# Tridiagonal form of a 256 x 256 matrix: turning A x instead of A u in the narrow half, and small steps moved from VectorE to GpSimd

## The chip, the cores and the metric

One core of a Trainium2 chip runs the whole kernel in one launch, all in float32. The metric is the device time of one execution in microseconds (us), as the median of several runs. Engines: TensorE (PE in the profile; its weight loads are PEld), VectorE (DVE), ScalarE (ACT), GpSimd (POOL), and SyncE (SP), which issues the DMAs.

## The reference, cut to what matters

Two graph layers are applied to 64 matrices x of 256 x 256, with one 256 x 256 adjacency matrix.

```python
def layer0(h, adj, S, W1, W2, W3):          # S = adj, so the weighting is adj * adj
    for each of the three weights: h = (adj * S) @ (h @ W), relu after the first two

def layer1(features, A, W1, b1, W2, b2):
    deg = sum(A, axis=0) + sum(A, axis=1) - diagonal(A)
    d_inv_sqrt = where(deg > 0, rsqrt(deg), 0)
    L_norm = d_inv_sqrt[:, None] * (diag(deg) - A) * d_inv_sqrt[None, :]
    _, U = eigh(L_norm)
    h = relu((U.T @ features) @ W1 + b1)
    return U @ (h @ W2 + b2)

x = x + layer0(relu(layernorm(x)), adj, adj, ...)
x = x + layer1(relu(layernorm(x)), adj, ...)
```

The expensive thing beside the matmuls is `eigh`: all eigenvectors of one symmetric 256 x 256 matrix. It depends on adj alone, not on x, so it can run beside layer 0.

## The kernel before, in words

**Two kinds of work run side by side.** The class `Eigen` computes the eigenvectors: the normed Laplacian (`laplacian`), its tridiagonal form by 254 Householder reflections (`tridiagonalize`, line 439), the reflections gathered into one matrix (`reflections`), the eigenvalues and eigenvectors of the tridiagonal matrix by divide and conquer from 16 small blocks up (`leaves`, then `level` for 32, 64, 128 and 256), and the products that give U and its transpose. This is one long chain of small dependent steps, most of them on VectorE. The class `Layers` works on the 64 matrices x in 32 pairs; its layer 0 (`products` and `rows`) is mostly matmuls on TensorE with copies on ScalarE, and needs nothing of the chain. Its layer 1 needs U, so it comes last.

**The class `Pace` (lines 161 to 259) mixes them by hand.** While the kernel is built, it keeps a clock of its own for each engine, with a cost for each operation (class `Op`). For every operation of the chain it works out when its inputs are ready, adds `LATER` (line 169: 0.4 us for TensorE, 0.1 for ScalarE), and lets waiting operations of layer 0 in ahead of it as long as they start before that (`chain`, `fits`, `run`). So the order of TensorE and ScalarE is fixed in the program. The order of VectorE, GpSimd and SyncE is set by the compiler's list scheduler, by its own times and in general by program order among what is ready. What is left of layer 0 when the chain ends is run at the start of layer 1 (`layer1`, `pace.finish`). The last pair's final steps are held back until then.

**One step of `tridiagonalize`** (k = 0 to 253, lo = k + 1) takes the current column x of A (below the diagonal) both as a row spread over all partitions, `xr`, and as a column, `xc` (two columns for the two halves of 128 rows). Rows are slices lo to 255, so they get shorter. Its parts:

- beta. `tail` is the sum of squares behind the first element (on ScalarE in the wide half, on VectorE in the narrow one), `nn` the squared length, `s0` its root on ScalarE. `q` is half the sign; `qn` = q nn; `qs` = q s0; `nb` = qn / s0 + qs, which is beta with its sign. In the trace `nb` is named m<-rs,qn,qs.
- A x as a column: `xa`, one row product with a sum for each half of 128 rows (r<-A,xr).
- u = x + beta e1: `u1` is its first element, written into `xr`; `uc` is the column. A u = A x + beta times the column of A at lo (`rc`): `ac`.
- The column `ac` is turned to a row on TensorE: a transpose of the column spread over 128 columns, into the PSUM tile psB (`pu`); the column `rc` is turned into psA (`pr`). One transpose each in the narrow half, two each in the wide one.
- `none` guards against a zero tail (two GpSimd operations), `den` = alpha beta + none, and `gam` = 1 / den. In the trace gam is a column of z.
- `gc` and `gr`: minus gam times A u as column and row. `uau` = u A u is a row product with a sum over pu and xr (r<-psB,xr). `c`, `f`: scalars out of it.
- The next column of A after the update, as a row (`both`, then `xn`) and as a column (`xcn`: two operations and a product with the 0/1 matrix `lower`), so that the next step's beta can be begun before A is updated.
- The update of A by two products of a row and a column for each half (A<-wr,q,A and A<-xr,wc,A).

For lo < 128 (127 steps) both halves of the rows are alive: this is the wide half. From lo = 128 on (127 steps) only the second half is alive: the narrow half. The helper `aside` puts q, qn, qs, gg = gam gam and gu = gg u1 on GpSimd in the wide half and on VectorE in the narrow one. The helpers `stt`, `ts`, `tt` and `recip` issue VectorE operations, so in the profile nearly all of them have line 209, where `Pace.issue` makes the call; steps are found by the names of tiles.

## Time and profile before

| what | value |
|---|---|
| median of 3 runs | 2453.63 us (2453.24 to 2455.24) |
| the profiled execution: its own time, its span | 2454.8 us, 2453.0 us |
| mean granted clock of TensorE | 0.99 |
| busy share of the span: PE, DVE, ACT, POOL | 98%, 88%, 41%, 19% |
| instructions of PE, DVE, ACT, POOL | 9240, 13352, 2827, 1625 |
| tridiagonal stage | from about 16 to 1348 us |
| last layer-0 matmul before layer 1; first DMA of layer 1 | 2242.52 us; 2272.59 us |

How to read it: the page gives the busy time of each engine, and the span in 40 slices with the busy share of each in tenths. PEclk is the clock that TensorE was granted, in tenths. A group of instructions is a line with the operation, its tiles (out<-in), its shape and count, then busy time in us and the mean of one in ns, then the idle time of the engine just before them and what ended it. A timeline line gives start and duration in us. A table of windows gives for each stretch the length and sum, then the busy time of PE, PEld, DVE, ACT and POOL with their instructions, the granted clock, the DMA share and GB/s. VectorE's instructions overlap: the next one may start while the last one writes, so a row of 0.30 us can be followed 0.21 us later by another one that doesn't need it. The spacing of starts is therefore what an operation costs its queue.

### The profile page before, as it was taken

The page shows a single profiled execution, that of the slowest core. Times are in us where ns is not written, and L with a number is a line of the kernel's source. Part 1 is how long each engine was busy: PE and PEld are TensorE (multiplying, and loading weights), DVE is VectorE, ACT ScalarE, POOL GpSimd, SP SyncE. Part 2 cuts the span into 40 slices and gives each one's busy share as a digit, 9 for nine tenths or more (in the row PEclk, how much of TensorE's full clock was granted, in tenths as well). Part 3 has the DMA queues.
Part 4 walks back from the last instruction along what each step waited for, and adds up shares of the span by engine and source line. Part 5 has one row for each costly group of instructions (what it writes and reads, how often), then busy time and mean ns, then how long its engine had stood idle before and what let it go on. Part 6 is the DMA issues. An engine that isn't in the chain of part 4 may idle for free. (4 is left out here: it accounts for less than half of the span.)

```text
span 2453.0 us, 38673 instructions
## 1 busy us (share of the span) xinstructions
PE 2393.1 (98%) x9240; PEld 1588.8 (65%) x9240; DVE 2151.1 (88%) x13352; ACT 1012.7 (41%) x2827; POOL 474.4 (19%) x1625
## 2 busy tenths in 40 slices
PE   7999999999999999999999999999999999997899
PEld 4666666666666656666666566666666666665788
DVE  7999999999999999999999999899987888786333
ACT  4344444544444444434444433334444444432222
POOL 2434333333333111111111000000000000000443
PEclk9999999999999999999999999999999999998899
DMA  3000000000000000000000000000000000000576
GB/s 112 18 13 15 22 23 18 22 22 23 6 22 23 23 18 23 22 22 6 23 23 23 30 22 23 9 18 23 22 22 27 18 22 22 22 5 1 202 257 202
DMA packets 59401, 90.05 MB, mean 37 GB/s; under 512 B 5792, under 2 KB 42784, under 8 KB 59168
## 3 DMA queue, kind: packets, MB, share of 16 engines
q1 hardware_dynamic: 59168, 87.52, 10.7%
q8 instruction: 75, 1.23, 0.2%
q14 instruction: 158, 1.29, 0.2%
HBM read 47.13 MB, written 40.37 MB: 36 GB/s over the span
## 5 line engine op out<-in xcount | busy, mean ns | idle before, releaser
L209 PE MATMUL bank<-y,L_gnn_W 128*128 128x512 f32 (+3 forms) x2184 | 905.5, 566 | 0.0
L209 PEld LDWEIGHTS bank<-y,L_gnn_W 128*128 128x128 f32 x2184 | 402.5, 190 | 436.1 <-issue 414.9
L209 PE MATMUL bank<-L_gnn_W,s 128*128 128x256 f32 (+1 forms) x2108 | 464.6, 374 | 6.0 <-ACT s L209 6.0
L209 PEld LDWEIGHTS bank<-L_gnn_W,s 128*128 128x128 f32 x2108 | 390.3, 191 | 56.1 <-ACT s L209 7.0
L209 ACT ACTIVATE s<-bank 128x512 f32<-128x512 f32 x384 | 224.7, 586 | 188.9 <-PE bank L209 187.7
L209 PE MATMUL bank<-gt,s 128*128 128x256 f32 (+1 forms) x1040 | 231.5, 376 | 0.0
L209 PE MATMUL bank<-L_gnn_W,y 128*128 128x512 f32 (+3 forms) x532 | 230.6, 578 | 0.0
L209 PEld LDWEIGHTS bank<-gt,s 128*128 128x128 f32 x1040 | 194.0, 190 | 35.9 <-issue 10.3
L209 ACT ACTIVATE s<-nn,guard 128x1 f32<-128x1 f32 x254 | 74.6, 294 | 238.3 <-DVE nn L209 214.6
L209 ACT COPY y<-bank 128x512 f32<-128x512 f32 x192 | 111.0, 581 | 132.4 <-PE bank L209 131.6
L209 POOL COPY m<-xr 128x1 f32<-128x1 f32 x254 | 55.2, 217 | 561.3 <-DVE xr L209 554.4
L209 PEld LDWEIGHTS bank<-L_gnn_W,y 128*128 128x128 f32 x532 | 98.7, 191 | 97.8 <-issue 95.0
L209 ACT ACTIVATE h<-x,shift,scale 128x256 f32<-128x256 f32 x256 | 137.5, 590 | 54.7 <-DVE shift L209 54.6
L209 ACT ACTIVATE junk<-x,nm 128x256 f32<-128x256 f32 x256 | 129.0, 504 | 31.3 <-DVE nm L209 27.3
L209 DVE SCALAR_TENSOR_TENSOR A<-xr,wc,A 128x255 f32<-128x255 f32 (+63 forms) x381 | 139.5, 367 | 0.0
L209 ACT ACTIVATE junk<-x 128x256 f32<-128x256 f32 x256 | 105.6, 412 | 80.9 <-DVE x L209 69.2
L209 ACT ACTIVATE junk<-xr 128x254 f32<-128x254 f32 (+63 forms) x127 | 46.0, 362 | 224.8 <-DVE xr L209 218.8
L209 DVE SCALAR_TENSOR_TENSOR A<-wr,q,A 128x255 f32<-128x255 f32 (+63 forms) x381 | 138.7, 365 | 0.0
L209 DVE SCALAR_TENSOR_TENSOR q<-q 128x1 f32<-128x1 f32 (+1 forms) x576 | 119.7, 208 | 15.0 <-ACT q L209 4.7
L209 PE MATMUL bank<-gt,h 128*128 128x256 f32 (+1 forms) x526 | 122.0, 381 | 2.3 <-ACT h L209 2.2
L209 PE MATMUL bank<-p,gt 128*128 128x512 f32 (+1 forms) x264 | 117.7, 580 | 0.0
L209 POOL TENSOR_TENSOR xb<-x,ub 128x512 f32<-128x512 f32 x16 | 19.9, 1267 | 500.8 <-DMA hw<-hw 489.7
(615 smaller groups left out, 4356.0 us busy)
## 6 DMA issues: line engine op xcount, KB each, us to landing
x<-x SPq DMA_DIRECT2D x60, 512.0 KB, 3.4
x<-in_x_dram SPq DMA_DIRECT2D x64, 256.0 KB, 3.6
out_dram<-out SPq DMA_DIRECT2D x64, 256.0 KB, 2.2
hw<-hw SPq DMA_DIRECT2D x60, 256.0 KB, 2.7
L_gnn_W<-in_L_gnn_W_dram SPq DMA_DIRECT2D x1, 2048.0 KB, 10.0
L_gnn_W<-in_L_gnn_W_dram SPq DMA_DIRECT2D x1, 1024.0 KB, 12.5
L_gnn_W<-in_L_gnn_W_dram SPq DMA_DIRECT2D x1, 512.0 KB, 5.2
mask<-in_c_blk_dram SPq DMA_DIRECT2D x2, 256.0 KB, 2.6
```

The costliest lines, as they stand in the source:

```text
L209: return op.call(*op.args, **op.kwargs)
```

## The change

In the narrow half (lo >= 128) the column A x (`xa`) is turned to a row (`px`) as soon as it is there, beside the way to beta; formerly A u (`ac`) was turned, which needs beta. gam A u is then put together both as a row and as a column from gam A x and gam beta times the column of A: `gnb` = gam nb; row `px1` = px gam, `gr` = pr gnb + px1; column `ac` = xa gam, `gc` = rc gnb + ac. `uau` is taken from `gr`, so it holds one gam more, and `gg` is gam itself there.

In the wide half the turned column is A u, as before.

In both halves q, qn, u1, gu and the product of `xcn` with `lower` are GpSimd operations now (q, qn and gu were so in the wide half already; qs stays on `aside`). In the wide half den becomes two GpSimd operations. gr and gc hold plus gam A u, so ngam goes and several sums become differences. uc is written in the living half alone, and the rest of `us` is set to zero once, ahead of the loop. The GpSimd memset of xcn's first column goes. LATER for TensorE is 0.5 instead of 0.4.

```diff
--- before.py
+++ after.py
@@ -166,7 +166,7 @@
 
     WINDOW = 1.0
     SLOWER, IN_BLOCKS = 1.06, 1.13
-    LATER = {"PE": 0.4, "ACT": 0.1}
+    LATER = {"PE": 0.5, "ACT": 0.1}
     HOP = 0.5
     LEAD = 1.5
 
@@ -449,6 +449,7 @@
         drow, erow = self.row("D"), self.row("E")
         nc.vector.memset(erow[:, N - 1 : N], 0.0)
         nc.vector.memset(us[:, :, N - 2 : N], 0.0)
+        nc.vector.memset(us[:, 0, P - 1 : N - 2], 0.0)
         nc.vector.memset(gams[:, N - 2 : N], 0.0)
 
         def as_row(tag, column, halves):
@@ -486,8 +487,8 @@
             x1 = xr[:, lo : lo + 1]
             self.stt(nn, x1, x1, tail, OP.mult, OP.add)
             nc.scalar.activation(s0, nn, AF.Sqrt, bias=guard)
-            aside(lo).tensor_scalar(q, x1, 0.0, 0.5, OP.is_ge, OP.subtract)
-            aside(lo).tensor_tensor(qn, q, nn, OP.mult)
+            nc.gpsimd.tensor_scalar(q, x1, 0.0, 0.5, OP.is_ge, OP.subtract)
+            nc.gpsimd.tensor_tensor(qn, q, nn, OP.mult)
             return nn, s0, q, qn
 
         xc = self.col("xc")
@@ -507,53 +508,69 @@
             self.recip(rs, s0)
             aside(lo).tensor_tensor(qs, q, s0, OP.mult)
             xa, junk = self.col("xa"), self.row("r0")
-            for h in halves:
-                self.stt(junk[:, r], a[:, h, r], 1.0, xr[:, r], OP.mult, OP.mult, accum=xa[:, h : h + 1])
-                if h == halves[0]:
-                    self.stt(nb, rs, qn, qs, OP.mult, OP.add)
+
 
             ac, uc = self.col("ac"), us[:, :, k]
-            self.stt(ac[:, hs], rc[:, hs], nb, xa[:, hs], OP.mult, OP.add)
-            pu, pr = as_row("psB", ac, halves), as_row("psA", rc, halves)
+            times_x = lambda h: self.stt(
+                junk[:, r], a[:, h, r], 1.0, xr[:, r], OP.mult, OP.mult, accum=xa[:, h : h + 1]
+            )
+            times_x(halves[0])
+            if lo >= P:
+                px, pr = as_row("psB", xa, halves), as_row("psA", rc, halves)
+            self.stt(nb, rs, qn, qs, OP.mult, OP.add)
+            if lo < P:
+                times_x(1)
+                self.stt(ac[:, hs], rc[:, hs], nb, xa[:, hs], OP.mult, OP.add)
+                pu, pr = as_row("psB", ac, halves), as_row("psA", rc, halves)
 
             none = self.col("none", 1)
             nc.gpsimd.tensor_scalar(none, tail, 1e-30, 1e30, OP.is_le, OP.mult)
             nc.gpsimd.tensor_tensor(none, none, nn, OP.add)
-            den, ngam, gg, gu = (self.col(c, 1) for c in ("den", "ngam", "gg", "gu"))
+            den, gg, gu = (self.col(c, 1) for c in ("den", "gg", "gu"))
             gam = gams[:, k : k + 1]
             u1 = xr[:, lo : lo + 1]
-            self.ts(u1, u1, nb, OP.add)
-            self.stt(den, alpha, nb, none, OP.mult, OP.add)
+            if lo < P:
+                nc.gpsimd.tensor_tensor(den, alpha, nb, OP.mult)
+                nc.gpsimd.tensor_tensor(den, den, none, OP.add)
+            else:
+                self.stt(den, alpha, nb, none, OP.mult, OP.add)
+            nc.gpsimd.tensor_tensor(u1, u1, nb, OP.add)
             self.recip(gam, den)
-            self.stt(uc, ident[:, :, lo], nb, xc, OP.mult, OP.add)
-            self.ts(ngam, gam, -1.0, OP.mult)
-            aside(lo).tensor_tensor(gg, gam, gam, OP.mult)
-            aside(lo).tensor_tensor(gu, gg, u1, OP.mult)
+            self.stt(uc[:, hs], ident[:, hs, lo], nb, xc[:, hs], OP.mult, OP.add)
             gc, gr = self.col("gc"), row("gr")
-            self.ts(gc[:, hs], ac[:, hs], ngam, OP.mult)
 
             uau, c = self.col("uau", 1), self.col("c", 1)
-            self.stt(junk[:, r], pu[:, r], 1.0, xr[:, r], OP.mult, OP.mult, accum=uau)
-            self.ts(gr[:, r], pu[:, r], ngam, OP.mult)
+            if lo < P:
+                nc.gpsimd.tensor_tensor(gg, gam, gam, OP.mult)
+                self.ts(gc[:, hs], ac[:, hs], gam, OP.mult)
+                self.stt(junk[:, r], pu[:, r], 1.0, xr[:, r], OP.mult, OP.mult, accum=uau)
+                self.ts(gr[:, r], pu[:, r], gam, OP.mult)
+            else:
+                gg, gnb, px1 = gam, self.col("gnb", 1), row("px")
+                self.tt(gnb, gam, nb, OP.mult)
+                self.ts(px1[:, r], px[:, r], gam, OP.mult)
+                self.stt(gr[:, r], pr[:, r], gnb, px1[:, r], OP.mult, OP.add)
+                self.stt(junk[:, r], gr[:, r], 1.0, xr[:, r], OP.mult, OP.mult, accum=uau)
+                self.ts(ac[:, hs], xa[:, hs], gam, OP.mult)
+                self.stt(gc[:, hs], rc[:, hs], gnb, ac[:, hs], OP.mult, OP.add)
+            nc.gpsimd.tensor_tensor(gu, gg, u1, OP.mult)
 
             xn, xcn, both, f = row("xr"), self.col("xc"), self.row("r1"), self.col("f", 1)
-            self.stt(both[:, rest], gr[:, rest], u1, pr[:, rest], OP.mult, OP.add)
-            self.stt(f, uau, gu, gr[:, lo : lo + 1], OP.mult, OP.add)
-            self.stt(xn[:, rest], xr[:, rest], f, both[:, rest], OP.mult, OP.add)
+            self.stt(both[:, rest], gr[:, rest], u1, pr[:, rest], OP.mult, OP.subtract)
+            self.stt(f, uau, gu, gr[:, lo : lo + 1], OP.mult, OP.subtract)
+            self.stt(xn[:, rest], xr[:, rest], f, both[:, rest], OP.mult, OP.subtract)
             more = lo + 1 < N - 1
             if more:
                 alpha1, tail1 = below(xn, lo + 1)
             self.stt(c, uau, 0.5, gg, OP.mult, OP.mult)
             wr, wc = row("wr"), self.col("wc")
-            self.stt(wr[:, r], xr[:, r], c, gr[:, r], OP.mult, OP.add)
-            self.stt(wc[:, hs], uc[:, hs], c, gc[:, hs], OP.mult, OP.add)
+            self.stt(wr[:, r], xr[:, r], c, gr[:, r], OP.mult, OP.subtract)
+            self.stt(wc[:, hs], uc[:, hs], c, gc[:, hs], OP.mult, OP.subtract)
             if more and halves[0]:
                 following = length(xn, lo + 1, tail1)
-            if halves[0]:
-                nc.gpsimd.memset(xcn[:, 0:1], 0.0)
-            self.stt(xcn[:, hs], gc[:, hs], u1, rc[:, hs], OP.mult, OP.add)
-            self.stt(xcn[:, hs], uc[:, hs], f, xcn[:, hs], OP.mult, OP.add)
-            self.tt(xcn[:, hs], xcn[:, hs], self.lower[:, hs, lo], OP.mult)
+            self.stt(xcn[:, hs], gc[:, hs], u1, rc[:, hs], OP.mult, OP.subtract)
+            self.stt(xcn[:, hs], uc[:, hs], f, xcn[:, hs], OP.mult, OP.subtract)
+            nc.gpsimd.tensor_tensor(xcn[:, hs], xcn[:, hs], self.lower[:, hs, lo], OP.mult)
             if more and not halves[0]:
                 following = length(xn, lo + 1, tail1)
 
```

## The prediction

> **What bounds the kernel now.** I read the page's slices first: who is busy, and where does that stop?
>
> ```profile
> span 2453.0 us, 38673 instructions
> ...
> PE   7999999999999999999999999999999999997899
> ...
> DVE  7999999999999999999999999899987888786333
> ...
> PEclk9999999999999999999999999999999999998899
> ```
>
> TensorE is busy nearly everywhere, because layer 0's matmuls are poured into the gaps of the eigenvector chain, and VectorE, which carries that chain, is busy for nine tenths of the time until slice 37. Both look like the bound. The table of windows (span; then PE, PEld, DVE, ACT, POOL busy; clock; DMA) tells them apart: tridiagonal form, wide half; narrow half; the place where the chain ends.
>
> ```profile
> 100.00:700.00 600.00, 599.09 (x2382) 390.77 (x2381) 578.30 (x3119) 288.17 (x872) 226.70 (x795) 1.00 0.06 20
> 800.00:1340.00 540.00, 536.16 (x2086) 345.17 (x2085) 522.84 (x4151) 233.92 (x637) 93.58 (x488) 1.00 0.06 20
> ...
> 2243.00:2278.00 35.00, 14.60 (x35) 10.36 (x35) 10.65 (x44) 9.60 (x30) 0.29 (x1) 0.57 0.10 35
> ```
>
> In the third row the poured-in work has run out (the last such matmul starts at 2242.52) while the chain has about 30 us to go: TensorE does 14.6 us of work in 35, at a clock of 0.57. So the chain sets the time today, but only just. If the chain gets shorter by X in the tridiagonal stage, the matmuls that no longer fit there move behind and fill this hole. Idle there: 35 - 14.6 = 20.4 us; and the work in it runs at about half clock: 14.6 x (1 - 0.57) = 6.3 us, if it stayed warm. So **a gain of the chain counts up to some 20 to 27 us; after that TensorE's own work is the bound** (in 2300 to 2450 it is busy for 148.38 of 150). A loss of the chain counts in full.
>
> Next the chain's step. The tridiagonal stage has 127 wide steps (lo < 128, from 20 to about 775 us) and 127 narrow ones (to 1348). In a narrow step around 1007 us the timeline (start, duration) shows
>
> ```profile
> 1007.40 0.22 DVE L209 SCALAR_TENSOR_TENSOR ac<-A,m,xa 128x1 f32<-128x1 f32 x1
> ...
> 1008.11 0.15 DVE L209 TENSOR_SCALAR ngam<-z 128x1 f32<-128x1 f32 x1
> 1008.18 0.15 DVE L209 TENSOR_TENSOR gg<-z 128x1 f32<-128x1 f32 x1
> ...
> 1008.36 0.27 PE L209 MATMUL psB<-ident,ac 128*128 128x128 f32 x1
> ...
> 1008.55 0.22 DVE L209 SCALAR_TENSOR_TENSOR xc<-gc,xr,A 128x1 f32<-128x1 f32 x1
> ...
> 1008.69 0.24 DVE L209 SCALAR_TENSOR_TENSOR r<-psB,xr 128x82 f32<-128x82 f32 x1
> ```
>
> The turned row is there at 1008.63, yet its reader (r<-psB) starts at 1008.69, when the last small operation ahead of it has gone. VectorE's own queue ends last. In the wide half it is another queue:
>
> ```profile
> 405.04 0.47 POOL L209 TENSOR_SCALAR q<-xr 128x1 f32<-128x1 f32 x1
> ...
> 405.59 0.46 POOL L209 TENSOR_SCALAR none<-m 128x1 f32<-128x1 f32 x1
> ...
> 406.13 0.21 POOL L209 TENSOR_TENSOR qn<-q,nn 128x1 f32<-128x1 f32 x1
> ...
> 406.63 0.39 POOL L209 TENSOR_TENSOR qs<-q,s 128x1 f32<-128x1 f32 x1
> ...
> 407.05 0.22 DVE L209 SCALAR_TENSOR_TENSOR m<-rs,qn,qs 128x1 f32<-128x1 f32 x1
> ```
>
> Beta (m<-rs,qn,qs) starts 0.03 us after GpSimd's qs, and GpSimd has had hardly a gap since 405.04. Stepping through all wide steps without layer-norm work, the median of that distance is 0.03 us. VectorE was idle for only 0.07 us per step there (6.9 us over 99), so the page does not name GpSimd; but it releases beta.
>
> **Narrow half, part by part** (by spacing of starts in the step from 1002.73 to 1007.15, 4.43 us long; it ends at beta). Leaves VectorE for GpSimd: q (0.07), qn (0.12), the product with lower (0.07), u1 (0.12), gu (0.12). Dropped: ngam (0.07), and gg (0.12), since gam takes its place: 0.69 us. Added on VectorE: gnb = gam beta (a single small operation like ngam, 0.07), and a row px1 = px gam (like gr<-psB, 0.21); gr becomes a two-operand row (0.22 for 0.21). That is -0.40 us. Against it, px1, gr and uau are now in series. A row that needs the one before it starts 0.34 us later (xr at 1005.41, tail at 1005.75) where the queue alone would take 0.21, so two gaps of 0.13; the small ac, gc, which depend only on gam and gnb, fit into them. Filled, the step wins 0.40; with both gaps open 0.14. The transposes now start from xa, beside beta, den, gam and gnb (0.25 + 0.26 + 0.26 + 0.19 = 0.96 us from beta's start). From ac's end to the row in PSUM it takes 1.01 us in the step above; from xa's end (1007.23), with LATER raised by 0.1, that is 1008.34, against 1008.11 for gam times beta: TensorE's row may end last, by some 0.2, which takes back part of the gain. On GpSimd the step has 8 operations instead of 4, at 0.21 to 0.25 each (its means in 800 to 1340), 1.8 us of 4.1: room, but qn and none are now queued behind each other ahead of beta and den; 0 to 0.15. I take **-0.25 us a step** (ends -0.40 and -0.10): 127 x 0.25 = 32 us less. Nothing on SP or the DMA queues is touched; GpSimd issues no DMA in this stage.
>
> **Wide half.** VectorE loses den (0.13), u1 (0.12), ngam (0.07) and the product with lower (0.07): 0.39 us. Two places must be kept apart.
> From beta to the row's reader: den becomes two GpSimd operations, each 0.19 like gg, and a hop of about 0.08: gam starts some 0.85 us after beta's start, 1.05 if u1 is queued between them, for 0.81 now (401.89 - 401.08). Behind gam wait gg, gc, gr. VectorE's queue there gets shorter by 0.32, but the turned row lands only 0.18 us before its reader starts (mean of the steps without layer norm), and LATER gives 0.1 of this away. So -0.18 to +0.20; I take -0.10, nearest to the queue's rows.
> From the new row x to the next beta: GpSimd ends last, and the product with lower joins this queue. In program order it stands ahead of q and qn and of the next step's none and qs, so I expect it before qs. What does it cost there? The groups by shape in 100 to 700 give both ends:
>
> ```profile
> L209 POOL TENSOR_SCALAR q<-xr 128x1 f32<-128x1 f32 x100 | 45.0, 450 | 0.0
> ...
> L209 POOL TENSOR_TENSOR gg<-z 128x1 f32<-128x1 f32 x99 | 19.1, 193 | 120.4 <-DVE z L209 120.4
> ```
>
> The same one-element work takes 450 ns while VectorE runs its long rows (q ends at 405.51, just after the update of A at 405.01 that lasts 0.42) and 193 ns beside VectorE's short ones. In between lie none (364), qs (374) and qn (222), the tensor operations of this very stretch; I take 0.30, less the 0.09 of idle that the queue has ahead of none (8.7 us over 100): +0.21. It is 0 if it lands behind qs, +0.45 if it waits out a row. Together **+0.11 us a step** (ends -0.18 and, both bad ends, +0.65): 127 x 0.11 = 14 us more.
>
> The Trainium skill, "SBUF — State Buffer", section "Who interferes with whom", says that a VectorE instruction with two SBUF inputs and a GpSimd instruction that reads SBUF exclude each other, and that the one issued first blocks the other. One direction is the 450 ns above. The other, VectorE waiting for GpSimd, the trace does not show: the row r<-A,xr at 406.29 starts inside qn's span (406.13 to 406.34) and takes 0.35, its usual 346 ns. By the rule the four operations newly on GpSimd (den twice, u1, the product with lower, 0.19 each) could each hold a row up, an estimated 0.76 us a wide step and 97 us in all; I go by the row.
>
> **Small things.** The memset of us (128 x 127) runs once, ahead of the loop: under 0.5 us, as the row copies there take 0.42. uc in the narrow half is one column instead of two: nothing, both take 0.2. Signs turned from add to subtract: nothing. The GpSimd memset of xc in the narrow half (98 ns) goes; it was idle time. LATER 0.4 to 0.5 lets layer-0 matmuls in for 0.1 us longer ahead of each step's first transpose: up to 254 x 0.1 = 25 us where TensorE's row ends last. Today it is covered by the 0.37 us (narrow) and 0.18 us (wide) that the row lies ready before it is read; in the changed narrow step that cover goes, and this is in the -0.10 end above.
>
> **Sum.** -32 + 14 = -18 us, under the 20 to 27 that the hole can give back, so all of it shows. The profiled execution took 2454.8 us (span 2453.0 and 1.8 around it), 1.2 more than the median of 2453.63. 2454.8 - 18 = 2436.8; as a median, 2436 us.
>
> **Rivals.**
> The hole closes. Narrow -0.40 and wide 0 would be X = 51 us, of which 20 to 27 show: 2427 to 2434, or, with TensorE waiting a little less for its transposes in 254 steps (0.05 each, 13 us), 2420 to 2429; I say 2427. For it: VectorE's 97% in the narrow half. Against it: GpSimd's queue in the wide half.
> GpSimd becomes the bound (the slower side). In the wide half beta waits for qs already; if the product with lower costs a full 0.45 in front of it, or den through two GpSimd operations and u1 comes late, so that the step gains 0.40, that is 127 x 0.40 = 51 us more, and 51 - 32 = 19 us slower: 2473. It decides from a loss of 0.25 us a wide step, which eats the 32 us of the narrow half. For it: 0.03 us between qs and beta. Against it: the front part's shorter queue.
> The change does not do what it says. TensorE's order is fixed when the kernel is built, with layer-0 work filled in by the kernel's own clock; if the transposes stand as far apart as before, VectorE only waits where it worked, and the step stays: 2449 to 2458, say 2452. For it: the transposes start more than 0.17 us after ac's end in 132 of 220 steps, so TensorE's order is near the edge too. Against it: that clock counts VectorE's operations, and they become fewer.
>
> **How the numbers follow.** Forecast (2429 to 2448): 0.40. Hole closed (2418 to 2429): 0.24. No change (2449 to 2458): 0.12. GpSimd the bound (2459 to 2485): 0.24. Faster by over 0.2% (below 2449; 0.2% is about what a measurement of this kernel can tell from no change): 0.64; within 0.2%: 0.12; slower: 0.24. The range 2420 to 2470 leaves out some 0.04 below and 0.13 above.
>
> **What would show it.** Narrow half: beta to beta at about 4.1 instead of 4.4 us, the row px1 starting about 0.9 us after beta, VectorE below 97% busy. Wide half: the product with lower on GpSimd ahead of qs, beta still 0.03 us behind qs, the new row x to the next beta longer by 0.2 (2.6 now); gam at 0.85 or more after beta. The stage ends at about 1330 instead of 1348, and the window in which TensorE idles at half clock shrinks from 35 us to 15 or less. The prediction is wrong if the wide step grows by 0.25 or more, if the narrow one does not shrink, or if the stage ends earlier and the end does not follow.

## The result

The changed kernel takes **2495.62 us** (median of four runs, 2492.24 to 2496.5) where the kernel before takes 2453.48 beside it (four runs, 2453.24 to 2455.24). The ratio is 1.0168, with an interval of 1.015 to 1.0185: slower by 1.7%, where 0.7% faster was forecast. The time lies above the range that ended at 2470.

The page of the changed kernel first; the lines answer to those of the kernel before.

```profile
span 2492.3 us, 39259 instructions
...
PE 2404.4 (96%) x9220; PEld 1576.2 (63%) x9220; DVE 2127.3 (85%) x12210; ACT 1012.6 (41%) x2827; POOL 655.6 (26%) x2641
...
PE   7999999999999999999999899999999999999899
...
DVE  7999999999999999989998999999898888786333
...
PEclk9999999999999999999999999999999999999999
```

VectorE did lose work (12210 instructions, formerly 13352) and GpSimd gained it (2641, formerly 1625), as the diff says. But VectorE's share fell from 88 to 85% while the span grew: it now waits. Where, the table of windows tells, with the same three stretches as in the prediction.

```profile
100.00:700.00 600.00, 593.85 (x2336) 382.12 (x2335) 556.46 (x2709) 282.84 (x858) 288.63 (x1187) 1.00 0.06 20
800.00:1340.00 540.00, 508.98 (x1950) 320.44 (x1949) 491.11 (x3287) 211.15 (x573) 176.85 (x904) 1.00 0.05 18
2243.00:2278.00 35.00, 35.00 (x92) 17.24 (x91) 29.80 (x151) 12.71 (x34) 0.00 (x0) 1.00 0.00 1
```

In the second row, the narrow half, VectorE idles for 540 - 491 = 49 us (17 before) and TensorE for 31 (4 before): each waits for the other, and neither is busy throughout. In the third row TensorE, which stood idle for 20 of 35 us there, works without a gap: the chain now ends later, and layer-0 work that found no place in the narrow half is done here.

Cutting the trace at the first beta, at beta of the first narrow step and at the last beta gives the two halves of the stage. The same cuts for all runs (stages and span in us from the profiled execution; median and ratio against the kernel before, run beside it):

| kernel | wide half | narrow half | last beta at | span | median | ratio (interval) |
|---|---|---|---|---|---|---|
| before | 766.1 | 559.8 | 1346.2 | 2453.0 | 2453.48 | |
| **after** | 767.2 | **595.2** | 1383.7 | 2492.3 | 2495.62 | 1.0168 (1.015 to 1.0185) |
| later_only | 769.6 | 562.5 | 1352.1 | 2461.5 | 2462.2 | 1.0035 (1.0021 to 1.0049) |
| moves_only | 768.0 | 534.5 | 1323.9 | 2441.5 | 2442.71 | 0.9955 (0.9938 to 0.9972) |
| turn_only | 760.5 | 608.8 | 1390.6 | 2499.2 | 2500.11 | 1.019 (1.0173 to 1.0207) |
| after_later04 | 767.5 | 585.5 | 1372.8 | 2491.1 | 2493.86 | 1.0168 (1.0151 to 1.0185) |
| rows_first | 767.6 | 548.7 | 1337.0 | 2443.2 | 2445.19 | 0.9969 (0.9957 to 0.9982) |
| rows_first_late | 766.8 | 606.7 | 1393.4 | 2496.5 | 2498.78 | 1.0193 (1.0176 to 1.021) |
| after_late | 767.3 | 614.2 | 1403.1 | 2502.9 | 2505.78 | 1.0221 (1.0204 to 1.0238) |
| moves_narrow | 761.1 | 535.5 | 1317.7 | 2424.9 | 2427.03 | 0.9899 (0.9882 to 0.9915) |
| rows_first_wr | 768.1 | 550.4 | 1341.0 | 2450.6 | 2448.88 | 0.9979 (0.9969 to 0.9988) |
| extra_row | 760.2 | 542.6 | 1322.9 | 2433.0 | 2433.94 | 0.9918 (0.9901 to 0.9935) |
| **lower_wide** | 752.6 | 534.2 | 1308.4 | 2423.7 | **2424.93** | 0.9881 (0.9864 to 0.9897) |
| qs_vector | 765.5 | 534.7 | 1320.3 | 2429.1 | 2431.66 | 0.9911 (0.9894 to 0.9928) |
| turned_repaired | 752.6 | 545.7 | 1318.4 | 2429.3 | 2431.69 | 0.9912 (0.9895 to 0.9928) |
| den_wide | 768.1 | 533.2 | 1321.1 | 2436.8 | 2440.38 | 0.9947 (0.993 to 0.9963) |

Of the 39.3 us that the span grew, 35.4 are the narrow half's (127 steps, 0.28 each), 1.1 the wide half's.

Two things are needed to read the stages. Each length is from one execution; versions whose code and LATER are the same in a half agree there within 2.3 us (narrow half of moves_only, moves_narrow, lower_wide, qs_vector and den_wide: 533.2 to 535.5) and 1.3 us (wide half of the changed kernel, after_late and the three rows_first versions: 766.8 to 768.1). And a version also differs in how much layer-0 work `Pace` lets into a stage. Counted from the traces in units of a 128x512 matmul (a 128x256 one is half a unit; the transposes to psA and psB are left out), it is

| kernel | wide half | narrow half |
|---|---|---|
| before | 1618 | 1211 |
| after, rows_first | 1600 | 1190 |
| after_later04 | 1582 | 1160 |
| moves_only | 1582 | 1161 |
| moves_narrow | 1614 | 1164 |
| lower_wide | 1592 | 1160 |
| turned_repaired | 1592 | 1166 |
| den_wide | 1595 | 1157 |
| qs_vector | 1622 | 1156 |
| extra_row | 1614 | 1174 |
| turn_only | 1614 | 1248 |

of 5184 units in the whole kernel, later layers included. Work that isn't done in the stage is done behind it, at an estimated 0.43 us a unit (925.5 units from 1800 to 2200 us in the kernel before, with TensorE busy for 399.82 of these 400). So a shorter stage is a gain of the kernel only where TensorE has idle time left behind it.

One narrow step of the changed kernel shows what happens. First TensorE, then VectorE (start, duration):

```profile
1004.16 0.29 PE L209 MATMUL psB<-ident,xa 128*128 128x128 f32 x1 [0.40 <-DVE m L209]
```

```profile
1003.93 0.21 DVE L209 SCALAR_TENSOR_TENSOR m<-rs,qn,qs 128x1 f32<-128x1 f32 x1
...
1004.51 0.16 DVE L209 RECIPROCAL z<-den 128x1 f32<-128x1 f32 x1
1004.71 0.16 DVE L209 TENSOR_TENSOR gnb<-z,m 128x1 f32<-128x1 f32 x1
1004.78 0.21 DVE L209 TENSOR_SCALAR ac<-xa,z 128x1 f32<-128x1 f32 x1
1005.02 0.22 DVE L209 SCALAR_TENSOR_TENSOR gc<-A,gnb,ac 128x1 f32<-128x1 f32 x1
1005.35 0.22 DVE L209 SCALAR_TENSOR_TENSOR xc<-gc,xr,A 128x1 f32<-128x1 f32 x1
1005.48 0.30 DVE L209 TENSOR_SCALAR px<-psB,z 128x86 f32<-128x86 f32 x1
1005.89 0.31 DVE L209 SCALAR_TENSOR_TENSOR gr<-psA,gnb,px 128x86 f32<-128x86 f32 x1
1006.23 0.25 DVE L209 SCALAR_TENSOR_TENSOR r<-gr,xr 128x86 f32<-128x86 f32 x1
```

The turned A x is in PSUM at 1004.45, half a microsecond after beta's start: turning it early works, and gam (z) is the last thing px needs. By 1004.71 VectorE has started gnb, which needs gam too, so px could run here. It starts at 1005.48. Ahead of it stand ac, gc and xc, and gc and xc each wait for the one before (0.24 and 0.33 between starts, where independent ones follow at 0.07 to 0.13). The row waits behind small operations that wait. Then px, gr and r<-gr,xr (which gives uau) wait for each other in turn, and nothing small is left to fill these gaps.

That is no single step. Over all 126 narrow steps from beta to beta, px starts ahead of gc in 9, and ahead of xc in 15. Over the steps without layer-norm work the median of the row's landing is 0.52 us after beta and that of px's start 1.56. And the groups in 800 to 1340 show VectorE's new idle time in front of just these lines (the last number is the idle time before them):

```profile
L209 DVE SCALAR_TENSOR_TENSOR gr<-psA,gnb,px 128x126 f32<-128x126 f32 (+56 forms) x114 | 33.0, 289 | 10.1
...
L209 DVE SCALAR_TENSOR_TENSOR xc<-gc,xr,A 128x1 f32<-128x1 f32 x114 | 25.0, 219 | 10.4 <-DVE gc L209 0.5
```

In the kernel before, xc<-gc had 0.0 there, and no row more than 5.5. One could instead look at TensorE's waits in the same stretch and blame the transposes:

```profile
PE psB L209 <- DVE r L209: 14.3, 32, 1.5
PE psB L209 <- DVE m L209: 13.5, 38, 0.7
```

TensorE waits 28 us for xa (r<-A,xr; m starts beside it), where the kernel before shows 2.8 us of waiting for psB's input in all. So there are two theories: **VectorE's order** (the row is read late), and **TensorE's lost time** (or LATER, which let the transposes come when they do). A third, from the prediction, is that the operations moved to **GpSimd** cost more than they save.

### The profile page after: what moved, and what is told of

Read it like the earlier page. It is cut to its first block, busy times and chain, and to the rows that moved or that the text cites. A ratio compares the mean times of both kernels' runs of the same rounds, so it can differ in the third digit from the quotient of the medians.

```text
span 2492.3 us, 39259 instructions
## 1 busy us (share of the span) xinstructions
PE 2404.4 (96%) x9220; PEld 1576.2 (63%) x9220; DVE 2127.3 (85%) x12210; ACT 1012.6 (41%) x2827; POOL 655.6 (26%) x2641
## 3 DMA queue, kind: packets, MB, share of 16 engines
q14 instruction: 164, 1.34, 0.2%
## 5 line engine op out<-in xcount | busy, mean ns | idle before, releaser
L209 POOL COPY zn<-q 128x32 f32<-128x32 f32 x32 | 7.0, 218 | 423.3 <-DVE q L209 370.6
## 6 DMA issues: line engine op xcount, KB each, us to landing
L_gnn_W<-in_L_gnn_W_dram SPq DMA_DIRECT2D x1, 1024.0 KB, 14.2
```

Source lines behind the costliest of these rows:

```text
L209: return op.call(*op.args, **op.kwargs)
```

## The experiments

### The parts apart

**later_only**: the kernel before, with only

```diff
-    LATER = {"PE": 0.4, "ACT": 0.1}
+    LATER = {"PE": 0.5, "ACT": 0.1}
```

> The kernel before with LATER 0.5 instead of 0.4 for TensorE, nothing else. The narrow step of before reads its turned row 0.44 us after it lands (median), so 0.1 us more should be hidden. Theory 'row order' (the changed narrow step is slower because VectorE's queue puts three small operations ahead of the row px, and px, gr, uau then follow one another): 2453 within 5 us. Rival 'LATER' (the later transposes cost the time): 2470 or more, with the narrow step 0.1 us longer.

Measured: 2462.2 us. LATER alone costs some 9 us, spread over the wide half (+3.5), the narrow one (+2.7) and what follows. That is more than the 5 I had allowed and far less than the rival needs.

**after_later04**: the changed kernel with this one line undone.

> The changed kernel with LATER 0.4. In the compiled queue of VectorE the row px stands ahead of the column xc in 41 of 122 narrow steps here, in 13 with 0.5. Theory 'row order': a little better than the changed kernel, 0.02 to 0.08 us a narrow step, 2485 to 2494. Rival 'LATER': back to 2453 within 5 us. Rival 'hops': 2495, no difference.

Measured: 2493.86 us. The narrow half gets 9.7 us shorter and the last beta comes 10.9 us earlier, but the span is only 1.2 us shorter: LATER is not the cause. Nothing arrives at the end because TensorE's own work is the bound there. The stage holds 48 units less layer-0 work, an estimated 21 us, and in 2200 to 2400 us TensorE is idle for 10.0 us in the changed kernel (first row) and for 1.4 here (second):

```profile
2200.00:2400.00 200.00, 189.98 (x779) 143.05 (x778) 109.48 (x384) 62.47 (x147) 42.34 (x34) 0.97 0.31 103
2200.00:2400.00 200.00, 198.56 (x804) 145.60 (x803) 104.00 (x370) 70.06 (x169) 42.48 (x35) 1.00 0.33 109
```

So the changed kernel stands near both bounds: the chain still ends last in it, but leaves TensorE idle for only 10 us there.

**moves_only**: the changed kernel, but A u is turned in the narrow half as before, and LATER is 0.4. Only the small operations are on GpSimd.

```diff
-            if lo >= P:
-                px, pr = as_row("psB", xa, halves), as_row("psA", rc, halves)
...
-            if lo < P:
+            if True:
                 nc.gpsimd.tensor_tensor(gg, gam, gam, OP.mult)
                 self.ts(gc[:, hs], ac[:, hs], gam, OP.mult)
```

> The changed kernel with A u turned in the narrow half as before and LATER 0.4: only the small operations are on GpSimd, in both halves. Theory 'row order': the narrow step gets shorter by some 0.2 us (VectorE's queue loses seven small operations), the wide one by nothing to -0.05: 2425 to 2445. Rival 'hops' (the small operations on GpSimd put their hops into the narrow step's path and leave VectorE without anything to fill its gaps): narrow step 0.15 us longer or more, 2470 to 2490.

Measured: 2442.71 us, the narrow half 534.5 (25.3 less than before, 0.20 a step). Moving small operations off VectorE is the good half of the change; GpSimd's queue is not the trouble in the narrow half. The span gains 11.5 us here, and 28.1 where den, u1 and the product with lower stay on VectorE in the wide half (moves_narrow, below).

**turn_only**: the changed kernel with the small operations back where they were, and LATER 0.4: A x is turned, nothing else.

```diff
-            nc.gpsimd.tensor_scalar(q, x1, 0.0, 0.5, OP.is_ge, OP.subtract)
+            aside(lo).tensor_scalar(q, x1, 0.0, 0.5, OP.is_ge, OP.subtract)
...
-            nc.gpsimd.tensor_tensor(u1, u1, nb, OP.add)
+            self.ts(u1, u1, nb, OP.add)
```

> The changed kernel with LATER 0.4 and the small operations where they were before (den, u1 and the product with lower on VectorE; q, qn, gu, qs on VectorE in the narrow half): only the turning of A x is left. Theory 'row order': the narrow step is as long as in the changed kernel or longer, 4.7 to 5.0 us against 4.44 before: 2485 to 2520. Rival 'hops': narrow step no longer than 4.45: 2455 or less.

Measured: 2500.11 us, the narrow half 608.8 (49 more than before). The turning costs what the change loses: +49.0 here, and +51.0 from moves_only to after_later04. In the narrow half the two parts of the change simply add.

### VectorE's order, or TensorE's lost time

**rows_first**: the changed kernel with three orders added to VectorE's queue, in the narrow half: ac behind px, gc behind gr, the first operation on xc behind uau. `behind(late, early)` fixes an order in the queue and nothing else: no engine waits for another by it. row1 is px1, row2 gr, row3 uau, first the operation xc<-gc,xr,A.

```diff
-                self.ts(ac[:, hs], xa[:, hs], gam, OP.mult)
-                self.stt(gc[:, hs], rc[:, hs], gnb, ac[:, hs], OP.mult, OP.add)
+                behind(self.ts(ac[:, hs], xa[:, hs], gam, OP.mult), row1)
+                behind(self.stt(gc[:, hs], rc[:, hs], gnb, ac[:, hs], OP.mult, OP.add), row2)
...
+            if lo >= P:
+                behind(first, row3)
```

> The changed kernel with three orders added to VectorE's queue in the narrow half, and no other edit: ac goes behind px, gc behind gr, the first column operation of xc behind uau. In the changed kernel px starts 1.56 us after beta (median) though its row has landed at 0.52 and gam is there at about 0.75. Theory 'row order': px starts at about 0.9, the narrow step falls from 4.74 to 4.1 to 4.3, and the time to 2430 to 2450. Rival 'rows in series' (px, gr and uau each wait for the one before, and what is taken out in front of them comes back as gaps between them and behind): narrow step 4.55 to 4.75, 2475 to 2496.

Measured: 2445.19 us, the narrow half 548.7. The order alone is worth 595.2 - 548.7 = **46.5 us**, with the same layer-0 work in the stage (1190 units). VectorE in one of its steps:

```profile
1017.13 0.21 DVE L209 SCALAR_TENSOR_TENSOR m<-rs,qn,qs 128x1 f32<-128x1 f32 x1
...
1017.72 0.15 DVE L209 RECIPROCAL z<-den 128x1 f32<-128x1 f32 x1
1017.90 0.16 DVE L209 TENSOR_TENSOR gnb<-z,m 128x1 f32<-128x1 f32 x1
1017.99 0.30 DVE L209 TENSOR_SCALAR px<-psB,z 128x80 f32<-128x80 f32 x1
1018.21 0.20 DVE L209 TENSOR_SCALAR ac<-xa,z 128x1 f32<-128x1 f32 x1
1018.39 0.30 DVE L209 SCALAR_TENSOR_TENSOR gr<-psA,gnb,px 128x80 f32<-128x80 f32 x1
1018.61 0.21 DVE L209 SCALAR_TENSOR_TENSOR gc<-A,gnb,ac 128x1 f32<-128x1 f32 x1
1018.81 0.24 DVE L209 SCALAR_TENSOR_TENSOR r<-gr,xr 128x80 f32<-128x80 f32 x1
```

px starts 0.86 us after beta (medians: 0.86 here, 1.56 in the changed kernel), and ac and gc lie in the gaps of the rows, each waiting for nothing: the picture that the prediction had in mind. TensorE's lost time vanishes by itself (narrow half, 800 to 1340):

```profile
800.00:1340.00 540.00, 536.89 (x2091) 346.90 (x2090) 507.08 (x3614) 235.89 (x639) 203.62 (x992) 1.00 0.06 20
```

**after_late**: the changed kernel with LATER 1.0 in the narrow half, so that layer-0 work fills TensorE until later. It gives TensorE its time back and leaves VectorE's order to the same scheduler.

```diff
+            if lo == P:
+                self.pace.LATER = {**self.pace.LATER, "PE": 1.0}
```

> The changed kernel with LATER 1.0 instead of 0.5 in the narrow half. Its row lands 1.04 us before it is read, so it can land 0.5 us later. Theories 'row order' and 'rows in series': narrow step 4.74 within 0.06, TensorE's idle time in 800 to 1340 us falls from 31 to under 15 us, the matmuls run out earlier at the end, and the time stays within 6 us of 2495. Rival 'lost TensorE time': 2480 or less.

Measured: 2505.78 us, where I had said 2495 within 6. TensorE's idle time in the narrow half falls from 34.7 to 3.5 us, and the kernel is 10 us slower: the time comes back as idle time behind the stage (66.5 us in 2200 to 2400). Lost TensorE time alone was not what cost. (My number for the step, 4.74, holds in the steps without layer-norm work; over all it is 4.87. Why the steps with layer-norm work lengthened was not settled.)

**rows_first_late**: rows_first with the same line.

> The same orders, and LATER 1.0 instead of 0.5 in the narrow half, so that TensorE takes up layer-0 work in place of waiting for xa. Theories 'row order' and 'rows in series': TensorE's idle time in the narrow half goes, but the row lands when it is wanted or 0.1 us after: narrow step 0 to 0.15 us longer than with the orders alone, time within 12 us of that. Rival 'lost TensorE time' (the 30 us that TensorE waits in the narrow half are what the change costs in the end): 15 us or more faster than with the orders alone.

Measured: 2498.78 us, 54 more than rows_first; I had expected it to stay near it. The narrow half's window says why:

```profile
800.00:1340.00 540.00, 539.99 (x2103) 353.26 (x2102) 468.51 (x3240) 233.77 (x630) 181.72 (x888) 1.00 0.06 21
```

TensorE is never idle and VectorE idles for 71.5 us: the turned row now comes 1.34 us after beta and px at 1.38. In the right order VectorE has no cover left for a late row. The early turning and a LATER that packs TensorE full work against each other.

### What the right order still lacks

**moves_narrow**: moves_only, with den, u1 and the product with lower back on VectorE in the wide half.

```diff
-                nc.gpsimd.tensor_tensor(den, alpha, nb, OP.mult)
-                nc.gpsimd.tensor_tensor(den, den, none, OP.add)
...
-            nc.gpsimd.tensor_tensor(u1, u1, nb, OP.add)
+            (nc.vector if lo < P else nc.gpsimd).tensor_tensor(u1, u1, nb, OP.add)
```

> Small operations on GpSimd in the narrow half alone; A u is turned in both halves, den, u1 and the product with lower are on VectorE in the wide half, LATER 0.4. If the wide half's moves cost 0.03 us a step, as its mean period says (5.997 before, 6.030 in the changed kernel, 6.031 with the moves alone), that is 4 us: 2436 to 2441, against 2442.7 with all the moves. Rival (the wide moves pay for themselves by what they leave free on VectorE): 2443 or more.

Measured: 2427.03 us, faster than both kernels and than I expected. The narrow half is 535.5 us, against 548.7 with A x turned and the rows first: even in the right order the turning seems to gain nothing. (LATER and the wide half differ here too; turned_repaired, below, leaves that out.)

**rows_first_wr**: rows_first, with c and wr also ahead of the new row xn, since in rows_first the second update of A had fallen behind rs in 80 of 126 steps (6 in moves_only).

```diff
+            if lo >= P:
+                wr = row("wr")
+                self.stt(c, uau, 0.5, gg, OP.mult, OP.mult)
+                ahead = self.stt(wr[:, r], xr[:, r], c, gr[:, r], OP.mult, OP.subtract)
+            new = self.stt(xn[:, rest], xr[:, rest], f, both[:, rest], OP.mult, OP.subtract)
+            if lo >= P:
+                behind(new, ahead)
```

> The changed kernel with the three orders in VectorE's queue and one more: in the narrow half c and the row wr come ahead of the new row x. With the three orders alone, beta to the new row is 2.33 us and from there to the next beta 1.91; with the small operations moved and A u turned, 2.55 and 1.58. Theory 'two more operations' (turning A x adds px and gnb to VectorE's queue, which is the narrow half's bound, and saves only a wait that was covered): 4.25 to 4.36 us a narrow step, still not below the 4.24 without the turning; 2432 to 2446. Rival 'order only' (with the right order the turning wins): 4.10 or less, 2428 or less.

Measured: 2448.88 us, the narrow half 550.4: no gain, outside what I gave. The order behind the rows is not what is missing, though this puts the update ahead of rs in 117 of 126 steps.

**extra_row**: moves_narrow with two operations more in each narrow step, a row and a small one of the kind that the turning adds. Nothing reads them.

```diff
+            if lo >= P:
+                gnb, px1 = self.col("gnb", 1), row("px")
+                self.tt(gnb, gam, nb, OP.mult)
+                self.ts(px1[:, r], pu[:, r], gam, OP.mult)
```

> The version with the small operations on GpSimd in the narrow half alone, and with two operations more on VectorE in each narrow step that nothing reads: a row (turned row times gam) and gam times beta, the two that the turning adds. Theory 'two more operations': 0.2 to 0.35 us a narrow step, 25 to 45 us more than the 2427 without them: 2450 to 2472. Rival 'gaps' (VectorE waits enough for such operations to vanish): 0.08 us or less, 2438 or less.

Measured: 2433.94 us, the narrow half +7.1, which is 0.06 us a step where the spacings of the two (0.21 and 0.07) make 0.28: the rival was right, they mostly go into gaps. Here they stand where nothing waits for them, so this prices two operations in the queue, not two in the path.

**turned_repaired**: the fastest placing of the small operations (lower_wide, below) with A x turned, and all four orders: px, gr, uau ahead of the small ones, c and wr ahead of xn. LATER is 0.4.

```diff
+            if lo >= P:
+                px, pr = as_row("psB", xa, halves), as_row("psA", rc, halves)
...
+                behind(self.ts(ac[:, hs], xa[:, hs], gam, OP.mult), row1)
```

> The fastest version so far (small operations on GpSimd, but den and u1 on VectorE in the wide half; A u turned; LATER 0.4; 2424.9) with A x turned in the narrow half and the four orders in VectorE's queue. Theory 'rows in series' (px, gr, uau one after another take as long as the wait for the row that they replace): narrow step 0.05 to 0.15 us longer than the 4.235 without turning, 2426 to 2440. Rival 'order only' (turning loses by the queue's order and by nothing else, and the wide half's moves hid it): narrow step 4.20 or less, 2424 or less.

Measured: 2431.69 us, the narrow half 545.7 against 534.2. The small operations are placed alike, so the turning, even in good order, costs **11.5 us** there and 6.8 in the time. The medians after beta, over the 86 steps without layer-norm work, say why it gains nothing. Without turning the row lands at 1.33, uau starts at 1.38 and the new row xn at 2.54. With it the row lands at 0.58, and px starts at 0.86, gr at 1.24, uau at 1.65, xn (with c and wr ahead of it) at 2.53. The row is read 0.5 us sooner, and px, gr and uau in series use that up: rs starts at 3.78 in both, and the median steps are 4.11 and 4.10. The loss is in the means: 0.05 us a step in these 86 (4.1 us), and 0.18 in the 40 steps with layer-norm work (7.4 us), where VectorE has more to do. What delays them there was not taken apart.

### The wide half

**lower_wide**: moves_narrow, with only the product with lower on GpSimd in the wide half too.

```diff
-            (nc.vector if lo < P else nc.gpsimd).tensor_tensor(xcn[:, hs], xcn[:, hs], self.lower[:, hs, lo], OP.mult)
+            nc.gpsimd.tensor_tensor(xcn[:, hs], xcn[:, hs], self.lower[:, hs, lo], OP.mult)
```

> The version with the small operations on GpSimd in the narrow half alone, and the product with lower on GpSimd in the wide half too. The prediction's term (it goes ahead of qs in the queue that releases beta, 0.21 us a step): 2450 or more. Theory 'small' (GpSimd catches up, because none behind it no longer meets a long row): 0.02 to 0.08 us a wide step, 2430 to 2438.

Measured: 2424.93 us, the wide half 752.6 against 761.1: 8.5 us shorter, where the prediction booked a loss of 0.21 a step. It is the fastest of all kernels here; moves_narrow, 2 us behind, is not told apart from it by their intervals. Of the 8.5 the span gets 1.2: the wide half holds 22 units less layer-0 work, an estimated 9 us that is done later, and TensorE is idle for 4.2 us in either version. So the run shows that the product with lower costs nothing on GpSimd; whether the step would be as much shorter with the same work beside it is not shown.

**den_wide**: moves_narrow, with den and u1 on GpSimd in the wide half.

> Small operations on GpSimd in the narrow half, and den and u1 on GpSimd in the wide half; the product with lower on VectorE in the wide half; A u turned, LATER 0.4. By difference of the stages of two versions (768.0 us with all the moves, 752.6 without den and u1) den and u1 on GpSimd cost 15 us in the wide half and some 10 us of TensorE's time there: the wide half 770 to 778 us, 2440 to 2452. Rival (the two moves only interfere with each other on GpSimd): wide half 755 to 764 us, 2432 or less.

Measured: 2440.38 us, the wide half 768.1: 7.0 us longer, and 15.4 where the product with lower is on GpSimd as well (752.6 to moves_only's 768.0). Both are longer with less layer-0 work in them (19 and 10 units), and TensorE's idle time in the wide half grows from 4.2 to 10.9 and 14.0 us: this loss is real, and the span is 11.9 us longer here than in moves_narrow. den and u1 were not moved one without the other.

**qs_vector**: moves_narrow, with qs on VectorE in the wide half.

```diff
-            aside(lo).tensor_tensor(qs, q, s0, OP.mult)
+            nc.vector.tensor_tensor(qs, q, s0, OP.mult)
```

> The version with the small operations on GpSimd in the narrow half alone, and qs on VectorE in the wide half: a single small operation (0.07 us) added to VectorE, and the last GpSimd operation ahead of beta gone. Reading 'GpSimd releases beta': the wide step gets 0.05 to 0.15 us shorter, 2408 to 2421. Rival (VectorE's queue is as late as GpSimd's there): no gain, 2424 to 2434.

Measured: 2431.66 us, the wide half 4.4 us longer (with 8 units more layer-0 work in it). The rival's number came, but the trace doesn't bear out its reason. In the wide steps without layer-norm work beta now starts 0.74 us after rs, where it was 0.84 (medians): GpSimd's qs did hold beta up, by 0.1. But the turned row lands 1.63 after beta instead of 1.50, its reader starts at 1.67 instead of 1.54, and the step stays (5.81 for 5.83). What kept the row from coming sooner was not taken apart.

## Why the prediction was wrong

**The bound, and what a loss costs: right.** That the chain sets the time, and a loss of it counts in full, held for the changed kernel: stage +37.5 us at the last beta, span +39.3. So did the cap on a gain, a little above the 20 to 27 that were said: in moves_narrow the last beta comes 28.5 us earlier and the span shrinks by 28.1; in lower_wide 37.8 earlier and 29.3. The last beta alone doesn't tell the time, though. In after_later04 it is 26.6 us later than before and the span 38.1 longer, since TensorE has lost time in the stage that no hole at the end gives back. Where the chain ends, TensorE is busy now. This is the window of lower_wide, with its clock at 1.00:

```profile
2225.00:2260.00 35.00, 34.61 (x163) 28.56 (x162) 5.47 (x12) 10.47 (x26) 9.90 (x8) 1.00 0.37 137
```

**Narrow half, the queue's sum: right in sign, far too large.** What VectorE sheds was 0.69 us a step by the spacing of starts. moves_only sheds just that, adds nothing, and gains 0.20. Less work in VectorE's queue pays only until something else ends last, and there that is mostly TensorE's row: psB lands at 1.33 after beta and uau starts at 1.38, where before it landed by 1.12 and uau started at 1.54 (medians over the steps without layer-norm work). The same shows from the other side in extra_row: 0.28 by spacing cost 0.06.

**Narrow half, the turning: wrong, and this is the step that failed.** The prediction says of the gaps between px1, gr and uau: "the small ac, gc, which depend only on gam and gnb, fit into them". Program order has the rows first, but in the queue as compiled ac, gc and xc stand ahead of px in nearly every step, and px starts at 1.56 after beta where about 0.9 was forecast. Instead of filling the rows' gaps they open gaps of their own (gc waits for ac, and xc for gc), and the rows' gaps stay open behind them. I had weighed "both gaps open" as the bad end, at a gain of 0.14; that the row would stand behind the small operations was not in my ends at all. The order costs 46.5 us. The whole narrow half, forecast at -32 us, is then 25.3 gained by the moves (559.8 to 534.5), 14.2 lost by the turning with the rows first (to 548.7; LATER goes to 0.5 in this step) and 46.5 lost by the order (to 595.2): +35.4. A bound on both sides has to include the bad order where a scheduler, not the program, sets it. The Trainium skill, "PSUM — Partial Sum Buffer", section "Engine vs sequencer instructions", says that the queues of ScalarE, VectorE and GpSimd are strictly first in, first out. The step at 1003.93 agrees: px has what it needs by 1004.71 and starts at 1005.48, after all that stands ahead of it.

Even put right, the turning loses 11.5 us of the narrow half (turned_repaired). In the kernel before, the wait for psB was covered by small operations (VectorE waited 1.0 us for it in 540); it ends last only once these are gone, and then the series of three rows takes the same time. Two more operations that nothing reads cost some 7 us (extra_row); whether they are the same microseconds was not shown.

**"TensorE's row may end last, by some 0.2": wrong** as things stand. It landed 1.03 us before it was read (median). It is what happens in rows_first_late.

**Wide half: inside its ends, both terms wrong.** Forecast +14 us, measured +1.1 (with 18 units less layer-0 work in it; it ends at 786 us before, not at the 775 of the prediction, on which nothing in its sum rests). From beta to the row's reader -0.10 was forecast, and it went from 1.58 to 1.57 us; from the new row to the next beta +0.21, and it went from 2.62 to 2.65 (medians over the steps without layer-norm work). That -0.10 and +0.21 both came to about nothing is luck for the sum. The product with lower was to cost 0.21 ahead of qs. It does stand there. GpSimd in one step of the changed kernel:

```profile
402.03 0.48 POOL L209 TENSOR_SCALAR q<-xr 128x1 f32<-128x1 f32 x1
402.47 0.19 POOL L209 TENSOR_TENSOR xc<-xc,lower 128x2 f32<-128x2 f32 x1
402.74 0.24 POOL L209 TENSOR_SCALAR none<-m 128x1 f32<-128x1 f32 x1
...
403.57 0.39 POOL L209 TENSOR_TENSOR qs<-q,s 128x1 f32<-128x1 f32 x1
```

But `none`, behind it, takes 0.24 where it took 0.46, and starts 0.27 after xc: from q's start to qs's start it is 1.54 us, and it was 1.59 (405.04 to 406.63) with one operation fewer. Over the whole wide half `none` takes 276 ns on average, where it took 422, the new operation takes 222, and from q to qs it is 1.61 us for 1.58 (medians). It looks as if the long part of `none` was waiting, which the new operation now does in its place; what it waited for is not shown. And my sign for den was wrong too. VectorE waits for it by name:

```profile
404.84 0.16 DVE L209 RECIPROCAL z<-den 128x1 f32<-128x1 f32 x1 [0.26 <-POOL den L209]
404.92 0.20 DVE L209 SCALAR_TENSOR_TENSOR ac<-A,m,xa 128x2 f32<-128x2 f32 x1
...
405.17 0.22 DVE L209 TENSOR_SCALAR gc<-ac,z 128x2 f32<-128x2 f32 x1
405.49 0.22 DVE L209 SCALAR_TENSOR_TENSOR xc<-gc,xr,A 128x2 f32<-128x2 f32 x1
```

gam starts 0.85 us after beta, as the prediction had it, and with it gc and xc slip behind the turned row's landing: uau starts at 1.57 (median), as before, and in lower_wide at 1.44. I had put this term at -0.10 because VectorE's queue was shorter; the queue's length counts for nothing once it waits for gam. With u1 it loses 15.4 us beside lower on GpSimd, 7.0 without. One way through the wide half is 766.1 before, 760.5 in turn_only (ngam and the memset of xcn's first column gone), 752.6 in lower_wide, 768.0 in moves_only, with den and u1 too. In another order the parts differ: with den and u1 already there (768.1), lower changes nothing.

**LATER: wrong.** "Today it is covered", I said; it costs 9 us in the kernel before.

**The rule of the Trainium skill's page "SBUF — State Buffer", section "Who interferes with whom",** that I set against the row: its estimate of 97 us did not come. With four operations more on GpSimd, VectorE's long rows kept their time: in 100 to 700 us r<-A,xr takes 347 ns on average (346 before), and the two updates of A 413 and 415 (411 and 413), with no idle time ahead of them in either kernel.

**The rivals.** "GpSimd becomes the bound" had the right sign and the wrong place: it was to cost 0.40 in the wide half, which lost 0.01. "The change does not do what it says" came closer in its words, "VectorE only waits where it worked", but I held TensorE's fixed order for the cause; it was VectorE's.

Still open: why the scheduler puts ac, gc and xc ahead of px. Only its result, the compiled order, was seen. What keeps the turned row back in qs_vector. And whether lower_wide has more in it: TensorE's own work is its bound where the chain ends, and no run here changed that work.

## What to carry to other kernels

An input that is ready earlier helps only if its reader's place in an in-order queue is earlier too: look up the compiled order of the reader's engine, and price the bad order as an end of the range. A wait that small operations already cover is worth little, and three dependent rows in its place cost what they take. Moving small operations from a crowded VectorE to GpSimd paid in the narrow half as a group (0.20 us a step, ngam's going included), and lost in the wide half where the chain waits for the result (den, moved with u1). And where one engine's spare work is filled into another's chain, count that work before a shorter stage is called a gain: lower_wide's 8.5 us came with fewer matmuls in the stage, and 1.2 us of them arrived at the end.

## What the runs showed of the hardware

- A short GpSimd operation can be free: with one more in the queue beside VectorE's long rows, the next one's mean fell from 422 to 276 ns, and from q to qs it was 1.61 us for 1.58.
- Two more operations on VectorE, 0.28 us by the spacing of their starts, cost 0.06 a step in a queue that was busy for 496 of 540 us (moves_narrow) and then for 511 (extra_row): VectorE's idle time there fell by 14 us, of some 34 that the two would ask for in 122 steps. Where the rest went is not shown.
- A row on VectorE started 0.34 to 0.42 us after the row it needs (px, gr and r<-gr,xr in the two steps above), even with a small operation between them; the prediction had taken 0.34 for all.
- GpSimd's qs released beta 0.03 us after its end in the wide half. Put on VectorE (qs_vector), beta came 0.10 us sooner after rs, and the step was no shorter: the turned row landed 0.13 later after beta.
- The Trainium skill, "Perfetto Trace Analysis", section "Optimizing Scalar/DVE Operations", warns that moving work from VectorE to GpSimd might not help, because they share a port. Here moving six kinds of small operations (and dropping ngam) gave 1.0 and 1.2% (moves_narrow and lower_wide).
